# Rows spread over 64 partitions by way of DRAM: one copy read in one transfer, or eight copies read in one transfer for each head

## The chip, the cores and the metric

The kernel runs on one core of one Trainium2 chip. The metric is the device time of one execution in microseconds. Before the change three runs took 3809.49, 3809.7 and 3804.15 us; their median is 3809.49 us.

The engines go by short names here: PE is TensorE's matmul, PEld its weight load, DVE is VectorE, ACT is ScalarE, POOL is GpSimd, SP is SyncE. A `q` behind a name (`SPq`, `POOLq`) is the engine's sequencer, which issues DMA transfers.

## The reference

The input is an image batch of shape 4 x 32 x 32 x 768 in float32. Two residual layers follow each other. Each normalizes its input by groups of channels, computes q, k and v, and lets every position of an image attend to all 1024 positions in 12 heads of 64 channels. The scores get a bias that depends on the row and the column distance of the two positions. The core of both layers, cut to what matters:

```python
attn = einsum('bqc,bkc->bqk', q * scale, k)
attn = attn + rel_h[..., :, None] + rel_w[..., None, :]
attn = softmax(attn, axis=-1)
o = attn @ v
x = x + o @ w_proj + b_proj
```

Layer 0 takes q, k and v straight from a product with a weight matrix. Layer 1 sends them through a 3x3 convolution of each channel and a layer norm first, and adds q to `o` before the last product.

## The kernel before, in words

The work is cut into 48 items. An item is one image, one layer and one pair of heads, which fill the 128 partitions with 2 x 64 channels. The order is: layer 0 of images 0 and 1, layer 1 of images 0 and 1, then the same for images 2 and 3, with six pairs in each. `attend` (L720) handles an item in two halves of 512 queries. For each half it goes over the 1024 keys in two groups of four tiles of 128: PE makes the scores (L873) and adds the bias by a second product with `ones` (L875), ACT takes the exponential (L880), and PE sums the weighted values (L897). Nothing is divided at that point. The values leave as `weighed`, and the sum of the exponentials is divided out later.

The program's order on PE, DVE, ACT and POOL is written out by hand: `attend` yields after each stretch of work, and at each yield the pieces of the next item (its products, convolutions, norms, `positions`, `split`) are put into the instruction streams at the steps that `plan` (L643) names. `more` (L731) takes the next part of the division from the list `rest`. Most items of layer 0 compute the q, k and v of neighbours by seven products of half size in place of eight (`sevens`, L391); their PSUM tiles are `m4m`, `m3m`, `m1m` and `m` in the trace, and DVE adds their results (L412). `positions` (L598) makes the products `rel` (L613) that the bias is taken from. SP issues its DMA transfers in the program's order: weights (L250 to L263, L275 to L291, L928 to L929), inputs and outputs (L964, L974), and the transfers `z_inv` (L844) and `t` (L850) of the division. Two buffers hold the weights of the products, so a weight load is issued when PE has finished with the one before the last.

The division needs one number for each query and head, and needs it on the 64 partitions of the head. There are two ways:

- **Layer 0** (44 of 48 halves). DVE adds the exponentials of the key tiles (L889, L891), PE sums them over the partitions into four groups of 32 partitions with 256 queries each (L792), ACT and DVE make the inverse on 256 columns (L798 to L829), and every 32nd partition of it is written to the DRAM tile `z_inv` by SP (L844 in `spread`). One step later `call` reads it back into all 128 partitions of `t` (L850), each head's row 64 times. `spread_finish` (L853) multiplies on DVE (L856) and adds the bias of v on ACT (L864).
- **Layer 1** (47 of 48 halves, `by_ones`). The value matrix has a column of ones, so the sums come out of PE in row 63 of each head. `copy` (L744) writes the two rows to the DRAM tile `z` (L753) and reads them back into `t` (L754), both from POOL's queue. ACT then starts the inverse with `sums` (L806, L814, L815), and DVE refines and multiplies (L828, L829, L834, L837). `restore_last` (L763) sends the row that the ones had taken (L776).

The tile `t` has one buffer, and the two DRAM tiles have two each. The four remaining halves of layer 0 and the last half of layer 1 sum on the partitions directly (L811) and use no DRAM.

POOL's queue also carries the bias. `split` (L624) cuts it into a high part, `high` (L629), and what is left, `whole` (L630), and issues 16 transfers of 128 KB for each item (L640), 8 for each half of the queries, the high part first.

In `t<-z` and `t<-z_inv` the source is written as `z.unsqueeze(1).to_broadcast([2, D, QC])`: 2 rows outermost, each repeated 64 times, 512 elements long. In the bias transfers it is `some.unsqueeze(1).to_broadcast([D // 2, 2, QC])`: 32 rows outermost, each repeated twice.

## Time and profile before

| | before |
|---|---|
| runs, us | 3809.49, 3809.7, 3804.15 |
| profiled execution, us | 3810.16 |
| its span, first to last instruction, us | 3808.1 |
| mean granted TensorE clock | 0.998 |
| DVE, ACT, POOL busy | 64%, 46%, 14% |
| DMA, mean over the span | 90 GB/s |
| HBM read, written | 195.76 MB, 40.28 MB |
| `t<-z` (POOL) | 47 transfers of 256 KB, 7.9 us to landing |
| `t<-z_inv` (SP) | 44 transfers of 256 KB |
| `z<-weighed`, `z_inv<-z_inv` | 47 and 44 transfers of 4 KB |
| bias (POOL) | 768 transfers of 128 KB, 2.9 and 3.2 us to landing |

The profile comes from one execution on the chip. Its page gives each engine's busy time and share of the span, then the span in 40 slices with the granted TensorE clock in tenths, then groups of instructions by line. `t<-z` reads "written from `z` into `t`", and `xN` counts instructions. A list of waits names an engine and its line, then what ended the wait, then the total in us, the number of waits and the longest. A timeline row gives the start in us from the span's start, the length in us, the engine, the line and what it did; idle time ahead of it stands in brackets with what ended it. A row of a table of windows gives the stretch, its length, each engine's busy us (with the number of instructions), the granted clock, the mean busy share of the 16 DMA engines and GB/s. The trace also holds a record of every DMA packet with its queue, start, length and size; these are called packet records below.

The issue of a DMA on SP or POOL shows as an instruction of about 0.5 to 0.8 us on that engine's sequencer. A transfer's landing is counted from its issue.

### The profile page before, as it was taken

Reading aid. Unit: us, or ns where it says so; the run is one execution under the profiler, and the core shown is the slowest. Engines: PE = TensorE matmul, PEld = TensorE weight load, DVE = VectorE, ACT = ScalarE, POOL = GpSimd, SP = SyncE. Lnnn points to the kernel's source line nnn. Section 1 sums busy time; section 2 is a strip of 40 time slices with the busy share of each in tenths; the row PEclk is TensorE's granted clock in tenths of the full one; section 3 lists DMA queues with packets and bytes.
Section 4 is the critical chain, followed back from the end, with each engine's and each line's share of the span. In section 5 each row is a group of like instructions: output and inputs, shape, how many; then the busy total and the mean of one; then the engine's idle time right before and its main releaser. Section 6 shows DMA issues by size and latency. Waiting matters only on the chain.

```text
span 3808.1 us, 76869 instructions
## 1 busy us (share of the span) xinstructions
PE 3734.4 (98%) x33166; PEld 1655.9 (43%) x33166; DVE 2440.7 (64%) x3068; ACT 1750.4 (46%) x2573; POOL 526.2 (14%) x964
## 2 busy tenths in 40 slices
PE   8999999999999999999999999999999999999998
PEld 4635535534344444444535455355343444434442
DVE  2556554559678877688454554445586888867874
ACT  2455424545255553455534544254453555525562
POOL 0111100111111211111200010001111112111120
PEclk9999999999999999999999999999999999999999
DMA  4444543331431223311334232523214212142123
GB/s 149 113 131 117 145 136 105 112 92 45 121 100 48 58 59 95 123 48 49 83 115 127 61 87 68 176 68 83 58 50 131 85 50 66 46 122 66 48 58 100
DMA packets 220097, 342.17 MB, mean 90 GB/s; under 512 B 50654, under 2 KB 104138, under 8 KB 219752
## 3 DMA queue, kind: packets, MB, share of 16 engines
q1 hardware_dynamic: 128984, 223.58, 18.7%
q0 software_dynamic: 90768, 113.61, 12.5%
q8 instruction: 264, 4.33, 0.5%
q14 instruction: 81, 0.66, 0.1%
HBM read 195.76 MB, written 40.28 MB: 62 GB/s over the span
## 4 chain that ended last, share of the span: by engine, by line
PE 45%; DVE 5%; ACT 1%; DMA 1%; issue 1%; POOL 0%; DVEq 0%; SPq 0%; ACTq 0%; POOLq 0%
PE qkv L131 9%; PE s L873 8%; PE av L897 8%; PE m4m L131 3%; PE m1m L131 2%; PE m3m L131 2%; PE s L875 2%; PE p3p L131 2%; PE p4p L131 2%; PE p1p L131 2%; PE rel L613 1%; PE m L131 1%; DVE shared L544 1%; PE ln_c L556 1%; DVE acc L891 1%
## 5 line engine op out<-in xcount | busy, mean ns | idle before, releaser
L880 ACT ACTIVATE e<-s 128x1024 f32<-128x1024 f32 x768 | 775.0, 1024 | 426.2 <-PE s L875 396.2
L131 PE MATMUL qkv<-xn,wqkv_t 128*64 128x512 f32 x3648 | 814.3, 595 | 7.1 <-DVE gmean L334 2.6
L873 PE MATMUL s<-q,k 64*128 64x512 f32 x3072 | 811.4, 604 | 6.3 <-ACT e L880 3.9
L544 DVE SCALAR_TENSOR_TENSOR shared<-shared,sm 128x1056 f32<-128x1056 f32 x576 | 757.9, 1316 | 15.6
L875 PE MATMUL s<-bias,ones 64*128 64x512 f32 x1536 | 613.8, 791 | 7.0 <-DMA bias<-whole 7.0
L897 PE MATMUL av<-e,vt 128*64 128x512 f32 x2624 | 596.3, 596 | 0.0
L131 PEld LDWEIGHTS qkv<-xn,wqkv_t 128*64 128x64 f32 x3648 | 256.1, 137 | 482.6 <-issue 464.7
L640 POOL DMA_DIRECT2D bias<-high x384 | 202.7, 548 | 1798.7 <-ACT high L629 1561.1
L891 DVE TENSOR_TENSOR acc<-acc,e 128x1024 f32<-128x1024 f32 x294 | 360.1, 1225 | 114.3 <-ACT e L880 87.4
L873 PEld LDWEIGHTS s<-q,k 64*128 64x128 f32 x3072 | 281.5, 186 | 265.0 <-issue 214.3
L527 ACT ACTIVATE shared<-qkv,sm 128x512 f32<-128x512 f32 (+1 forms) x288 | 129.1, 501 | 467.9 <-PE qkv L131 467.9
L897 PEld LDWEIGHTS av<-e,vt 128*64 128x64 f32 x2624 | 185.6, 137 | 350.1 <-issue 317.5
L875 PEld LDWEIGHTS s<-bias,ones 64*128 64x128 f32 x1536 | 149.5, 187 | 191.3 <-issue 188.5
L640 POOL DMA_DIRECT2D bias<-whole x384 | 207.2, 571 | 48.2 <-DVE whole L630 31.1
L747 ACT COPY weighed<-av 128x512 f32<-128x512 f32 x96 | 56.3, 586 | 299.9 <-PE av L897 299.9
L559 DVE TENSOR_REDUCE mean<-ln_c 128x8 f32<-128x512 f32 x144 | 98.6, 685 | 107.5 <-PE ln_c L556 107.5
L889 DVE TENSOR_TENSOR acc<-e 128x1024 f32<-128x1024 f32 x49 | 60.0, 1224 | 167.6 <-PE z L792 128.0
L776 POOL DMA_DIRECT2D weighed<-last x94 | 50.6, 540 | 682.1 <-ACT last L773 679.1
L613 PEld LDWEIGHTS rel<-q,rel 64*32 64x32 f32 x6144 | 111.8, 105 | 58.8 <-issue 54.8
L613 PE MATMUL rel<-q_t,rel 64*32 64x32 f32 x6144 | 123.5, 195 | 2.5 <-issue 2.5
L613 PE MATMUL rel<-q,rel 64*32 64x32 f32 x6144 | 122.5, 195 | 0.8 <-issue 0.8
L131 PE MATMUL m3m<-xn,wqkv_t 128*64 128x512 f32 x528 | 120.9, 592 | 2.3 <-DVE shared L412 2.3
(172 smaller groups left out, 4289.3 us busy)
## 6 DMA issues: line engine op xcount, KB each, us to landing
bias<-high POOLq DMA_DIRECT2D x384, 128.0 KB, 2.9
bias<-whole POOLq DMA_DIRECT2D x384, 128.0 KB, 3.2
wqkv_t<-in_wqkv SPq DMA_DIRECT2D x78, 384.0 KB
wqkv_t<-mixed SPq DMA_DIRECT2D x66, 384.0 KB
wproj_t<-mixed SPq DMA_DIRECT2D x48, 384.0 KB
wqkv_t<-in_wqkv SPq DMA_DIRECT2D x66, 192.0 KB
xn<-in_x SPq DMA_DIRECT2D x24, 512.0 KB
x<-in_x SPq DMA_DIRECT2D x48, 256.0 KB
```

The lines of the kernel that those rows point to most:

```text
L131: nc.tensor.matmul(ps[lo : lo + D], a[:, lo : lo + D], b, start=start, stop=stop, **kw)
L527: nc.scalar.activation(self.pad[s][:, rows, there : there + src.shape[2]], src, AF.Identity, bias=col(self.column(s)))
L544: nc.vector.scalar_tensor_tensor(y, window, tap, y, ALU.mult, ALU.add)
L559: nc.vector.tensor_reduce(of, heads, AX.X, ALU.add)
L613: nc.tensor.matmul(ps[lo : lo + S, k * S : (k + 1) * S].rearrange("p (b c) -> p b c", b=2), rel[rows, 2 * self.layer + i, first : first + ...
L640: nc.gpsimd.dma_start(sets, some.unsqueeze(1).to_broadcast([D // 2, 2, QC]))
L873: nc.tensor.matmul(ps[:, j, :], k[rows, keys], q[rows, cols], start=True, stop=False)
L875: nc.tensor.matmul(ps[:, j, :], ones[rows, kt % 2 * P : (kt % 2 + 1) * P], bias[c][rows, kt // 2, :], start=False, stop=True,)
L880: nc.scalar.activation(e, ps, AF.Exp)
L889: nc.vector.tensor_tensor(acc, es[0], es[1], ALU.add)
L891: nc.vector.tensor_tensor(acc, acc, e, ALU.add)
L897: nc.tensor.matmul(av[j * D : (j + 1) * D, :], pair.vt[:, kt, j * D : (j + 1) * D], e[:, j, :], start=(kt == 0), stop=(kt == NKT - 1),)
```

## The change

Both DRAM tiles, `z` and `z_inv`, become eight times as large: `[2, 8, 512]` instead of `[2, 512]`. The writes fill all eight copies from the same rows. For `z` this stays one transfer; for `z_inv` it becomes one for each head, because the row of a head comes from two partitions with 256 columns each. The new helper `spread_rows` reads a head's eight copies into that head's 64 partitions, each copy eight times, and is called with POOL's queue in `copy` and with SP's in `call`. So `t` is filled by two transfers of 128 KB in place of one of 256 KB, and their source is 8 (repeated) x 8 copies x 512 elements. No arithmetic is changed, and nothing is moved to another step.

```diff
+COPIES = 8
...
+    def spread_rows(queue, t, z):
+
+        for j in range(2):
+            there = z[j].unsqueeze(0).to_broadcast([D // COPIES, COPIES, QC])
+            queue.dma_start(t[j * D : (j + 1) * D, :], there)
...
-                z = dram.tile([2, QC], F32, tag="z", name="z", bufs=2)
-                nc.gpsimd.dma_start(z, weighed[D - 1 :: D, :])
-                nc.gpsimd.dma_start(t, z.unsqueeze(1).to_broadcast([2, D, QC]))
+                z = dram.tile([2, COPIES, QC], F32, tag="z", name="z", bufs=2)
+                nc.gpsimd.dma_start(z, weighed[D - 1 :: D, :].unsqueeze(1).to_broadcast([2, COPIES, QC]))
+                spread_rows(nc.gpsimd, t, z)
...
-                z = dram.tile([2, QC], F32, tag="z_inv", name="z_inv", bufs=2)
-                nc.sync.dma_start(z.rearrange("j (h x) -> (j h) x", h=2), inv[S - 1 :: S, :])
+                z = dram.tile([2, COPIES, QC], F32, tag="z_inv", name="z_inv", bufs=2)
+                for j in range(2):
+                    rows = inv[(2 * j + 1) * S - 1 : (2 * j + 2) * S : S, :]
+                    there = z[j].rearrange("r (h x) -> h r x", h=2)
+                    nc.sync.dma_start(there, rows.unsqueeze(1).to_broadcast([2, COPIES, QC // 2]))
...
-                nc.sync.dma_start(t, z.unsqueeze(1).to_broadcast([2, D, QC]))
+                spread_rows(nc.sync, t, z)
```

## The prediction

> **What bounds the kernel now.** I read the page's busy shares first, then the PE waits, then who waits for the row transfers that the change touches, then the windows and the timeline around those waits.

> ```profile
> PE 3734.4 (98%) x33166; PEld 1655.9 (43%) x33166; DVE 2440.7 (64%) x3068; ACT 1750.4 (46%) x2573; POOL 526.2 (14%) x964
> ...
> PEclk9999999999999999999999999999999999999999
> ```

> TensorE is busy 98% of a span of 3808.1 us, so the change, which removes no matmul, can win only from the 74 us in which PE stands, and from its clock. The first 14 us of these are the first load. The PE waits (total us, times, longest) name most of the rest:

> ```profile
> PE warm L319 <- DMA xn<-in_x: 13.9, 1, 13.9
> ...
> PE s L875 <- DMA bias<-whole: 7.0, 4, 2.9
> ...
> PE rel L613 <- issue: 3.3, 3, 2.5
> ...
> PE m3m L131 <- DVE shared L412: 2.3, 1, 2.3
> ```

> No PE wait names the tile `t`. Its other waiters do, in DVE's and ACT's wait lists:

> ```profile
> DVE t L856 <- DMA t<-z_inv: 36.2, 6, 7.4
> ```

> ```profile
> ACT inv L806 <- DMA t<-z: 1.9, 1, 1.9
> ```

> How the transfer moves now stands in windows that hold little else (the last two columns are the mean busy share of the 16 DMA engines and GB/s). The first has `t<-z_inv` alone, the second only bias transfers:

> ```profile
> 276.00:279.80 3.80, 3.80 (x20) 1.29 (x18) 0.70 (x2) 0.00 (x0) 0.00 (x0) 1.00 0.13 51
> ...
> 3288.00:3290.50 2.50, 2.50 (x14) 0.86 (x12) 2.43 (x4) 0.00 (x0) 2.50 (x6) 1.00 0.92 250
> ```

> 0.13 of 16 is two engines: the 256 KB, whose source has 2 rows outermost, crawl on two engines at 25 GB/s each. The bias transfers, 32 rows outermost, use all 16. The issue table says the same: `t<-z` 256 KB lands in 7.9 us, bias 128 KB in 2.9 to 3.2. The packet records of `t<-z_inv` show 128 packets of 2 KB, 0.085 us each, 64 in a row on each of two engines: 5.4 us.

> **Where this reaches PE.** Six times `t<-z_inv` is issued just as the 16 bias transfers go out, and shares its two engines with them. It then lands 10.0 to 11.0 us after its issue (packet records) instead of 6.5 to 7.8, DVE stands for it, and the bias transfers, which use the same two engines among their 16, land in 6 to 8 us. One of the six in the timeline, PE's row and DVE's (start, length, and in brackets the idle time before and what ended it):

> ```profile
> 254.71 0.50 PE L875 MATMUL s<-bias,ones 64*128 64x512 f32 x2 [2.35 <-DMA bias<-whole]
> ```

> ```profile
> 259.14 0.69 DVE L856 TENSOR_TENSOR t<-weighed,t 128x512 f32<-128x512 f32 x1 [4.08 <-DMA t<-z_inv]
> ```

> The four bias waits of PE are 0.74 (385.05), 2.35 (254.71), 2.92 (2142.10) and 0.98 (2581.88). The last three lie behind such a collision; at 385 the transfer, issued at 382.93, was not yet moving. After the two long ones the clock falls:

> ```profile
> 255.00:260.00 5.00, 5.00 (x20) 2.65 (x17) 0.75 (x2) 3.07 (x3) 0.90 (x2) 0.66 0.65 196
> ...
> 1818.00:1823.00 5.00, 3.82 (x14) 2.24 (x16) 4.76 (x10) 1.30 (x4) 5.00 (x11) 0.66 0.97 242
> 2143.00:2148.00 5.00, 5.00 (x25) 2.48 (x22) 0.69 (x1) 3.13 (x4) 0.52 (x1) 0.66 0.33 78
> ```

> 5 us at 0.66 is 1.7 us lost. Waits of 0.98 and 2.34 us left it at 1.00 in their windows.

> **The change, part by part.** *The read of `t`.* Two transfers of 128 KB, each with 8 rows outermost, repeated, in place of one of 256 KB. No row has 8. From the side of speed the bias row bounds a half at 2.9 us; from the other, 7.9 us as now. I take about 3.4 for both halves, 2.9 and one further issue of 0.5: if the engines used follow the outermost rows, as with 2 and 32, 8 engines at 25 GB/s carry 128 KB in 0.64 us. [...]

> *The write of `z` and `z_inv`.* 16 packets of 2 KB, or two transfers of 16 of 1 KB, for 2 or 4 packets. If one row stays on one engine, 8 packets of 0.085 us: +0.6 us; between 0 and +1.5, what the bias row of 3.2 lies above the 1.7 of `z`. Taken: 0.6 on POOL, 0.4 on SP.

> *Issues.* SP has two more per use (0.52 each), 44 times, and waits for the second write: `t` is issued some 1.0 us later on SP and 0.6 on POOL, its second half 0.5 later still. Behind the waiting SP stand the halves of `t`, then weight loads. In the common pattern (274.42) SP's next issue follows 5.4 us later and itself waits for PE, which covers it. At six places (447.67, 527.65, 892.88, 1970.06, 2412.02, 2777.89) it follows after 0.6 to 2.4 us; were the weights there just in time, that is 6 x 1.5 = 9 us, but PE's only wait for weights in the whole run is 0.9 us. POOL has 47 issues of 0.84 turned into two of about 0.55, and a `z` write of 0.58 or a little more: 0.3 to 0.6 us, ahead of issues that come 5 us later (idle 4.95 before `weighed<-last` at 1806.26). Both at nothing.

> *The gains, in terms.*
> 1. Bias waits. PE needed the bias at 252.36, 2139.18 and 2580.90; the last transfer of that half was issued at 248.7, 2135.5 and 2577.2. With the undisturbed 3.2 us it is there at 251.9, 2138.7 and 2580.4, ahead each time; with 16 packets of `t` on an engine in front (16 x 0.085 = 1.4) up to 0.9 late. So 6.25 us are won at best, 3.55 at worst; I take the middle, 4.9.
> 2. The clock behind the two long ones: 2 x 1.7 = 3.4.
> 3. At 394 DVE stood 5.79 us for `t`, and PE's m3m then 2.34 for DVE. `z_inv` left at 379.87; 3.1 us to the first read today, 1.0 for the longer front, then 1.75 to the first packet and twice 1.4 us of packets shared with bias give 388.5 to 389 against DVE's readiness at 388.68: 2.3 won.
> 4. At 1807.81 ACT waited 1.85 us for `t<-z`. Its twin at the end of the other half of the batch did not wait:

> ```profile
> 1807.81 0.63 ACT L806 ACTIVATE inv<-t 128x512 f32<-128x512 f32 x1 [1.85 <-DMA t<-z]
> ...
> 3683.92 0.63 ACT L806 ACTIVATE inv<-t 128x512 f32<-128x512 f32 x1
> ```

> PE then stood 2.47 us ahead of `rel` (1810.18), in the twin 0.53, and the clock fell in the first place only: 1.94 + 1.7 = 3.6. With the change `t` lands by 1804.6 (issue 1801.1, then 3.4), before ACT is free at 1805.96. What is late next there is ACT's own chain, as in the twin.

> Sum 4.9 + 3.4 + 2.3 + 3.6 = 14.2 us. The profiled execution took 3810.16, so 3796.0; the median of the runs, 3809.49, lies 0.7 lower: **3795.3**.

> **The rivals.**
> *Bias is its own bound.* The 16 bias transfers hold 0.92 of the engines by themselves; terms 1 and 2 might stay, only 3 and 4 come: 3809.5 - 5.9 = 3803.6. For it: the 0.92. Against it: undisturbed bias lands in 2.9 to 3.2.
> *The halves aren't spread* (copies folded into one source, or placed on the same two engines). If the longer front is hidden too, the time stays 3809.5. If it isn't, *slower*: `t` lands 1.5 us later at five places where it already binds (the three bias waits, m3m, 1808), so 7.5 us, and the waits of 0.98 and 2.34 us grow into clock falls, 3.4 more: 3820. This decides as soon as the landing of `t` passes today's. For it: no row shows 8. [...]

> **How the numbers follow.** 0.2%, 7.6 us, is about what a measurement of this kernel can tell from no change. Forecast 0.64, bias its own bound 0.16, not spread and hidden 0.10, not spread and slower 0.10. The forecast's own range is 3790 to 3802: all of term 1 and 2 us of other waits more, or half of the terms. The range reaches to the bias rival and stops short of the slow one: 3789 to 3807. Faster 0.64, same 0.26, slower 0.10.

> **What would show it.** In windows with `t` alone a DMA share of about 0.5 instead of 0.13; `t<-z` landing in about 3.4 us; DVE's wait for `t<-z_inv` down from 36.2 us to under 4; PE's for bias under 3.5; no 0.66 at these three places; ACT at 1808 not waiting. It is wrong if `t` lands as late as today, or if PE waits for weights.

## The result and the profile after

| | before | after |
|---|---|---|
| median of 8 runs each, us | 3808.89 | 3793.51 |
| lowest to highest, us | 3804.15 to 3811.64 | 3790.87 to 3797.78 |
| profiled execution and its span, us | 3810.16, 3808.1 | 3790.87, 3788.9 |
| PE standing still, gaps over 0.15 us, us | 65.8 | 55.7 |

The ratio is 0.9964, with a 95% interval of 0.9955 to 0.9973: faster by 0.36%, or 15.4 us between the medians where 14.2 were forecast. Line numbers are 3 to 12 higher in the changed kernel (L613 is now L616, L856 is L868, L875 is L887, L806 is L815); its reads of `t` are L725.

The page of the kernel after, the lines that answer to those shown of before:

```profile
PE 3725.5 (98%) x33166; PEld 1651.2 (44%) x33166; DVE 2442.2 (64%) x3068; ACT 1750.2 (46%) x2573; POOL 545.0 (14%) x1011
...
PEclk9999999999999999999999999999999999999999
```

Its list of waits (engine, line, what ended the wait, then total us, times, longest):

```profile
PE warm L322 <- DMA xn<-in_x: 12.4, 1, 12.4
...
DVE t L868 <- DMA t<-z_inv: 9.1, 5, 2.7
...
PE rel L616 <- issue: 2.2, 1, 2.2
...
PE s L887 <- DMA bias<-whole: 1.6, 1, 1.6
```

DVE's wait for `t` fell from 36.2 to 9.1 us and PE's for bias from 7.0 to 1.6; m3m and ACT's `inv` no longer wait. The `rel` wait is still there, and it says "issue", not the name of an engine: this matters below. PE is busy 8.9 us less with the same 33166 matmuls, of which the clock explains most.

The read of `t` by itself, on POOL's queue, in the windows table (busy us of PE, PEld, DVE, ACT, POOL, then granted clock, DMA share, GB/s). First before, in a window in which almost every packet belongs to one `t`:

```profile
1301.00:1305.00 4.00, 3.76 (x24) 2.01 (x24) 3.90 (x6) 3.57 (x5) 0.00 (x0) 1.00 0.14 56
```

then after, in a window that holds nothing but the 64 packets of two halves:

```profile
1184.60:1186.20 1.60, 1.60 (x10) 0.31 (x6) 0.67 (x2) 0.00 (x0) 0.00 (x0) 1.00 0.51 146
```

0.14 of 16 engines is two. The 0.51 is an average, and the eight has to be read from the packet records of this window: eight packets of 4 KB are under way while one half moves, and 16 to 18 for the 0.3 us in which both do. So each half moves on eight engines, and on POOL's queue the second half uses eight others than the first. The issue tables, before and then after (size, median us from issue to landing), show what that does to one transfer:

```profile
t<-z POOLq DMA_DIRECT2D x47, 256.0 KB, 7.9
...
z<-weighed POOLq DMA_DIRECT2D x47, 4.0 KB, 1.7
```

```profile
t<-z POOLq DMA_DIRECT2D x94, 128.0 KB, 3.2
...
z<-weighed POOLq DMA_DIRECT2D x47, 32.0 KB, 2.3
```

The packet records agree: after an issue before, there are 64 packets of 4 KB and 448 of 8 bytes, which fits 32 for each of 14 engines that carry nothing; after, the two halves leave 64 of 8 bytes, which fits 4 for each of 8 idle engines, twice. On SP, 2 packets of 2 KB were under way at once (3 at most), now 8 (10 at most). It stays at 8 where both halves are issued together (at 849.3), so there they share the same eight. The prediction's estimate, worked out from the 2 and the 32 rows of before, held: here 8 rows outermost gave 8 engines.

The stall shown at 254.71 has shrunk to nothing for PE. DVE's timeline of after (start, length, idle time before in brackets) at the same multiply:

```profile
253.88 0.69 DVE L868 TENSOR_TENSOR t<-weighed,t 128x512 f32<-128x512 f32 x1 [0.59 <-DMA t<-z_inv]
```

and the windows of after near the three places where the clock had been at 0.66 (the whole trace of after has no fall of the clock but the one at the program's end):

```profile
254.00:259.00 5.00, 5.00 (x32) 1.73 (x32) 4.25 (x4) 3.03 (x8) 0.00 (x0) 1.00 0.75 231
...
1818.00:1823.00 5.00, 3.58 (x20) 1.33 (x19) 4.24 (x9) 3.64 (x6) 1.14 (x2) 1.00 0.18 33
2141.00:2146.00 5.00, 5.00 (x26) 1.72 (x24) 1.59 (x4) 2.89 (x4) 0.00 (x0) 1.00 0.16 44
```

**Where 19.2 us of span went.** PE's gaps are 10.1 us shorter and its busy time 8.9. Of the gaps, 5.4 are bias waits (three gone, 6.25; that at 385 grew by 0.85), 2.3 m3m, 0.7 net the two ends of layer 1, 1.5 the first load. Of the busy time, 6.8 are four falls of the clock that are gone (at 256, 1819, 2143 and 3754), each recorded as 3.413 us at half speed, so 1.7 lost. This execution is the fastest of the eight after, and the medians differ by 15.4 only: the first load and two of the four falls come and go, as the experiments show.

### The profile page after: what moved, and what is told of

Its sections match the earlier page's. It is cut to its first block, busy times and chain, and to the rows that moved or that the text cites. A ratio compares the mean times of both kernels' runs of the same rounds, so it can differ in the third digit from the quotient of the medians.

```text
span 3788.9 us, 77201 instructions
## 1 busy us (share of the span) xinstructions
PE 3725.5 (98%) x33166; PEld 1651.2 (44%) x33166; DVE 2442.2 (64%) x3068; ACT 1750.2 (46%) x2573; POOL 545.0 (14%) x1011
## 3 DMA queue, kind: packets, MB, share of 16 engines
q1 hardware_dynamic: 130832, 224.84, 19.2%
## 4 chain that ended last, share of the span: by engine, by line
PE 88%; DVE 8%; ACT 2%; issue 1%; DMA 1%; SPq 0%; POOL 0%; DVEq 0%; ACTq 0%
PE qkv L134 19%; PE s L885 16%; PE av L909 16%; PE m4m L134 5%; PE m1m L134 5%; PE m3m L134 5%; PE s L887 4%; PE p3p L134 3%; PE p4p L134 3%; PE rel L616 3%; PE p1p L134 2%; PE m L134 2%; DVE shared L547 2%; PE ln_c L559 1%; DVE acc L903 1%
## 5 line engine op out<-in xcount | busy, mean ns | idle before, releaser
L887 PE MATMUL s<-bias,ones 64*128 64x512 f32 x1536 | 611.3, 789 | 1.6 <-DMA bias<-whole 1.6
L887 PEld LDWEIGHTS s<-bias,ones 64*128 64x128 f32 x1536 | 148.6, 187 | 184.1 <-issue 176.3
L616 PEld LDWEIGHTS rel<-q,rel 64*32 64x32 f32 x6144 | 111.7, 105 | 60.6 <-issue 56.5
L616 PE MATMUL rel<-q,rel 64*32 64x32 f32 x6144 | 122.4, 195 | 2.4 <-issue 2.2
L616 PE MATMUL rel<-q_t,rel 64*32 64x32 f32 x6144 | 123.4, 195 | 0.0
L134 PE MATMUL m4m<-xn,wqkv_t 128*64 128x512 f32 x528 | 121.7, 596 | 1.5 <-ACT z_inv L808 1.4
```

The lines of the kernel that those rows point to most:

```text
L134: nc.tensor.matmul(ps[lo : lo + D], a[:, lo : lo + D], b, start=start, stop=stop, **kw)
L616: nc.tensor.matmul(ps[lo : lo + S, k * S : (k + 1) * S].rearrange("p (b c) -> p b c", b=2), rel[rows, 2 * self.layer + i, first : first + ...
L887: nc.tensor.matmul(ps[:, j, :], ones[rows, kt % 2 * P : (kt % 2 + 1) * P], bias[c][rows, kt // 2, :], start=False, stop=True,)
```

## The experiments

**Theory:** `t` is slow because 2 rows outermost hold it at two engines, and these two also delay the bias transfers; the rows outermost are what counts, and the gain comes at the SP reads of layer 0 (terms 1 to 3) and the POOL reads of layer 1 (term 4). **Rivals:** the copies help, because 64 partitions no longer read one address; two transfers in flight help; or one half of the change does everything. All ratios are to the kernel before on the same chip, whose median was 3805.98, 3807.95 and 3806.23 us on the three chips used (E1 to E4, E5 to E8, E9 to E11).

**E1 and E2, each half alone.** E1 leaves POOL's `z` and `t` as they were, E2 SP's.

```diff
 E1
-                z = dram.tile([2, COPIES, QC], F32, tag="z", name="z", bufs=2)
-                nc.gpsimd.dma_start(z, weighed[D - 1 :: D, :].unsqueeze(1).to_broadcast([2, COPIES, QC]))
-                spread_rows(nc.gpsimd, t, z)
+                z = dram.tile([2, QC], F32, tag="z", name="z", bufs=2)
+                nc.gpsimd.dma_start(z, weighed[D - 1 :: D, :])
+                nc.gpsimd.dma_start(t, z.unsqueeze(1).to_broadcast([2, D, QC]))
```

> Only layer 0's transfers are changed (z_inv in eight copies, t<-z_inv as two transfers); layer 1's z and t are as before. Theory (t leaves its two engines, so bias and DVE no longer wait): the bias waits of PE stay near 1.6 us, DVE's wait for t<-z_inv near 9 us, the wait of 2.34 us at m3m is gone, so 7.7 us of stalls plus clock falls: about 3798 us, 11 us under before, and ACT's 1.85 us wait at the end of layer 1 is back. Rival (layer 1's half is what counts, by the end of each half of the batch): 3804 or above.

> Only layer 1's transfers are changed (z in eight copies, t<-z as two transfers); layer 0's are as before. Theory: ACT's wait of 1.85 us goes, PE wins 1 to 2 us there and perhaps one clock fall of 1.7 us: 3805 to 3808 us; the bias waits of 7.0 us, DVE's 36 us and m3m's 2.34 us stay. Rival: most of the gain is here, 3798 us.

E1 took 3795.97 us, ratio 0.9977 (0.9968 to 0.9986), 10.0 us won. E2 took 3803.97, ratio 0.9991 (0.9982 to 1.0), 2.0 us won, which is at the edge of what can be told from nothing. The waits of E1:

```profile
DVE t L868 <- DMA t<-z_inv: 8.6, 5, 2.4
ACT inv L815 <- DMA t<-z: 2.3, 1, 2.3
PE rel L616 <- issue: 2.3, 2, 2.0
...
PE s L887 <- DMA bias<-whole: 0.7, 1, 0.7
```

and of E2:

```profile
DVE t L865 <- DMA t<-z_inv: 35.8, 6, 7.6
...
PE s L884 <- DMA bias<-whole: 5.2, 3, 2.4
PE rel L616 <- issue: 3.0, 2, 2.5
PE m3m L134 <- DVE shared L415: 2.6, 1, 2.6
```

Each half removes its own waits and leaves the other's. The `rel` line is new knowledge: in E1 ACT waits 2.3 us for `t<-z` and PE stands 2.0 there, in E2 ACT does not wait and PE stands 2.5. PE's `rel` wait does not come from ACT's.

**E3, one copy, 64 rows outermost.** The writes are those of before; each head's single row is read 64 times with the repetition outermost.

```diff
-            there = z[j].unsqueeze(0).to_broadcast([D // COPIES, COPIES, QC])
+            there = z[j : j + 1, :].to_broadcast([D, QC])
```

> z and z_inv stay single copies written as before; only the read is cut into two transfers, one for each head, each with 64 repeated rows outermost, so that all rows of a transfer read the same 2 KB. Theory (the outermost dimension sets the engines, not the addresses): 64 on both sides gives 16 engines, t lands about as early as with eight copies or earlier, and one write of 4 KB is shorter than what eight copies need: 3790 to 3794 us. Rival A (the copies matter, reads of one address queue up): t lands in 6 us or more and the time goes back towards 3805 or above. Rival B (splitting by head alone is what helps): the same time as with eight copies, but a DMA share that stays at two engines.

3793.82 us, ratio 0.9973 (0.9963 to 0.9982), 12.2 us won: the whole gain of E1 and E2 together, without any copy. Its issue table and waits:

```profile
t<-z POOLq DMA_DIRECT2D x94, 128.0 KB, 2.8
...
z<-weighed POOLq DMA_DIRECT2D x47, 4.0 KB, 1.7
```

```profile
DVE t L865 <- DMA t<-z_inv: 1.1, 1, 1.1
PE s L884 <- DMA bias<-whole: 0.8, 1, 0.8
```

A half lands 0.4 us earlier than with eight copies, the front is shorter, and DVE's wait falls to 1.1 us. No packet of 8 bytes is recorded, which fits 16 engines that all carry. So reading one row 64 times does not undo the gain, and the rival of the addresses falls as the cause. It is not free: with four copies, 16 rows outermost (E8), a half lands in 2.5 us, 0.3 earlier, and most often 16 of its packets are under way at once, where with one copy it is mostly 6 to 13. In the kernel's time this can't be seen.

**E4, 32 copies.** Only `COPIES = 32`, which makes 2 rows outermost again.

> The changed kernel with 32 copies in place of eight: two transfers again, but the source is 2 (repeated) x 32 copies x 512. Theory: back to two engines, each transfer of 128 KB at 51 GB/s, and a longer write: t lands as late as before or later, DVE's wait for t<-z_inv is 36 us or more, PE's bias waits 6 us or more: 3808 to 3822 us. Rival A (different addresses are what helps): as fast as with eight copies, 3794 us. Rival B (the split by head helps): also near 3794 us.

3886.87 us, ratio 1.0217 (1.0203 to 1.0231): 81 us slower, far beyond what was expected, 3822 at most. Two engines came back as expected (448 packets of 8 bytes, 5.9 us for each half), but the write of `z` grew as well (128 KB, 4.4 us), and then SP's order did damage that the prediction had put at nothing. SP's timeline of E4:

```profile
706.44 1.08 SPq L856 DMA_DIRECT2D z_inv<-z_inv  x2
711.68 0.50 SPq L725 DMA_DIRECT2D t<-z_inv  x1
726.79 0.34 SPq L266 DMA_DIRECT2D wqkv_t<-mixed  x1
727.18 0.52 SPq L725 DMA_DIRECT2D t<-z_inv  x1
```

DVE and PE in the same stretch:

```profile
733.08 0.69 DVE L868 TENSOR_TENSOR t<-weighed,t 128x512 f32<-128x512 f32 x1 [19.73 <-DMA t<-z_inv]
```

```profile
738.22 4.53 PE L134 MATMUL m3m<-xn,wqkv_t 128*64 128x512 f32 x10 [8.90 <-DVE shared L415]
```

The second half of `t` stands behind a weight load (L266) that SP could not issue for 14.6 us; SP's waits name PE's m3m matmuls as what usually holds L266. DVE waits 19.7 us for that half, and PE in turn 8.9 for DVE. The span is 75.0 us longer than before's: PE's gaps make 52.5 of it (three such circles of 8.7 to 8.9 us, and bias waits of 22.9 in all), and its busy time 22.5, with 13 falls of the clock against 4. E4 changes engines, write and order at once, so it doesn't price the two engines alone; E7 and E9 do.

**E5 and E11, the changed kernel again**, on two other chips:

> The changed kernel unchanged, on the same chip as its neighbours here. Theory: 12 to 16 us under before on this chip, ratio 0.996 to 0.997. A ratio beside that of the single-copy kernel (0.9973) within the intervals would say that the copies themselves bring nothing.

> The changed kernel, unchanged, beside the one with a single copy on one chip: ratio 0.995 to 0.9975. The clock falls near 1803 and near 3680 to 3755 come and go between executions if they are not tied to t; if they are tied to it, none is seen there.

3792.54 us, ratio 0.9954 (0.994 to 0.9968), and 3792.41, ratio 0.996 (0.9946 to 0.9974). The bias wait at 380 is 0.7 us in both, as before the change, so the 1.6 of the first execution is no effect of it. The clock near 1801 and 3680, in the windows of E5 and then of E11:

```profile
1801.00:1806.00 5.00, 3.86 (x41) 1.94 (x41) 4.76 (x5) 4.91 (x7) 0.69 (x2) 1.00 0.02 3
3676.00:3682.00 6.00, 4.48 (x18) 2.33 (x18) 5.76 (x10) 2.75 (x5) 6.00 (x13) 0.72 0.97 227
```

```profile
1799.00:1806.00 7.00, 4.72 (x54) 2.40 (x42) 6.53 (x8) 6.50 (x9) 0.98 (x2) 0.64 0.02 5
3676.00:3682.00 6.00, 4.47 (x18) 2.15 (x16) 5.72 (x11) 2.27 (x5) 6.00 (x13) 0.72 0.94 223
```

One kernel, three executions: at 1801 no fall, no fall, a fall of 6.8 us; at 3678 none, one, one. PE stood the same 2.2 to 2.3 us at `rel` each time. The falls at the ends of layer 1 are therefore not tied to `t`. The two behind the bias waits (256 and 2143) are: none of the eight executions with SP's reads on 8 or 16 engines has one there. With the slow read such falls stay, but they change places: at 254, 400 and 701 in E2, at 2269 in E7, at 2266 in E9, each time at a bias or m3m wait.

**E6, eight copies in one transfer.**

```diff
-                spread_rows(nc.sync, t, z)
+                nc.sync.dma_start(t, z.unsqueeze(2).to_broadcast([2, COPIES, D // COPIES, QC]))
```

(and the same on POOL's queue)

> z and z_inv in eight copies as in the change, but t is read in one transfer of 256 KB with 2 rows outermost, each of the eight copies eight times: other addresses, same outermost dimension as before. Theory (engines): t stays on two engines at 51 GB/s, its front is longer by 0.5 to 1 us, DVE's wait for t<-z_inv stays at 36 us or grows to 45, the bias waits stay: 3806 to 3818 us. Rival A (reading eight addresses is what helps): as fast as the change, about 3793 us.

3793.03 us, ratio 0.9957 (0.9943 to 0.9971). The premise of the expectation failed: this does not hold the read at two engines. The issue table and a window that holds only one such transfer:

```profile
t<-z POOLq DMA_DIRECT2D x47, 256.0 KB, 3.2
```

```profile
1292.70:1293.70 1.00, 1.00 (x12) 1.00 (x10) 0.80 (x2) 0.60 (x1) 0.00 (x0) 1.00 0.62 225
```

0.62 on average is more than 8 of 16, up to 18 packets are under way at once, and the read leaves no 8-byte packet (the 56 of each use belong to the write of `z`): [2 heads][8 copies] lie one behind the other in DRAM and act as 16 rows. So E6 is no test of the addresses (E3 is). It shows that the split into two transfers isn't needed: DVE's wait is 4.9 us, against 9.4 for the changed kernel on this chip, and the times agree within their intervals. On 16 engines each, the kernel took 3793.03 us with one transfer and 3792.51 with two (E8). The split gains nothing here; what the copies bring is more engines, as the 7.7 us of the same write read from copy 0 alone (E9) beside the 3.2 here show.

**E7, the split alone.** Two copies, outermost, each repeated 32 times, in one transfer for each head.

```diff
-COPIES = 8
+COPIES = 2
...
-            there = z[j].unsqueeze(0).to_broadcast([D // COPIES, COPIES, QC])
+            there = z[j].unsqueeze(1).to_broadcast([COPIES, D // COPIES, QC])
```

> Two copies, and two transfers of 128 KB, one for each head, with the 2 copies outermost, each repeated 32 times: the change's split, but with 2 outermost. Theory (engines): each half runs on two engines, 51 GB/s, on SP both on the same two, and where weight loads slip in between the halves the second half is later still: t as late as before or later, 3806 to 3840 us. Rival B (the split by head is what helps): as fast as the change, about 3793 us.

3813.19 us, ratio 1.001 (1.0001 to 1.0019). DVE's wait is 38.4 us, PE's for bias 8.8 and for m3m 4.8, and 448 packets of 8 bytes are back:

```profile
t<-z POOLq DMA_DIRECT2D x94, 128.0 KB, 5.2
```

```profile
DVE t L868 <- DMA t<-z_inv: 38.4, 6, 7.1
```

Two transfers on two engines each were no better here than one.

**E8, four copies**, so 16 rows outermost (`COPIES = 4`):

> The changed kernel with four copies: 16 (repeated) x 4 copies x 512, so 16 outermost and a shorter write. Theory: 16 engines, t<-z lands in 2.8 to 3.2 us, DVE's wait for t<-z_inv falls from 9 us to 1 to 5 us, the time is that of eight copies or up to 3 us less. Rival (a larger number of copies is what helps): slower than with eight copies, by a part of the gain, 3797 to 3802 us.

3792.51 us, ratio 0.9957 (0.9943 to 0.9971); a half lands in 2.5 us, `z` in 2.0, DVE waits 2.0 us. 16 engines were worth no more than 8 for the time (3792.54 in E5, on the same chip): what PE still waits for isn't `t`.

**E9, the new write with the old read**, from copy 0:

```diff
-                spread_rows(nc.sync, t, z)
+                nc.sync.dma_start(t, z[:, 0, :].unsqueeze(1).to_broadcast([2, D, QC]))
```

(and the same on POOL's queue)

> The new write (eight copies, and its second issue on SP) with the old read of 256 KB in one transfer from copy 0, 2 rows outermost. Theory (the 2 rows outermost hold the read at two engines, whatever the copies): t<-z lands in 7.9 us as before, DVE's wait for t<-z_inv is 36 us or up to 6 us more for the later issue, PE's bias waits 7 to 9 us, m3m 2.3 to 4, ratio 1.000 to 1.003. Rival (the longer front costs at five places 1.5 us each and two clock falls): ratio 1.003 or more. Rival (the copies themselves help): bias waits under 4 us and ratio 0.998 or less.

3808.54 us, ratio 1.0007 (0.9998 to 1.0016). `t<-z` lands in 7.7 us, DVE waits 42.6 us, and the waits of PE only move (7 to 9 us were expected for bias, 2.3 to 4 for m3m):

```profile
PE s L887 <- DMA bias<-whole: 5.2, 2, 4.4
PE m3m L134 <- DVE shared L415: 4.6, 3, 2.2
```

The copies and their second write on SP cost between nothing and 0.16% by themselves; the rival's 0.3% or more is excluded.

**E10, one copy beside the changed kernel on one chip:**

> The kernel with one copy and 64 repeated rows outermost once more, now on one chip with the changed kernel. Theory (the copies bring nothing, the rows outermost do): within 0.1% of the changed kernel's ratio, DVE's wait for t<-z_inv at 0 to 3 us against its 9. Rival (the copies are worth something beyond the engines): slower than the changed kernel by more than 0.1%.

3792.72 us, ratio 0.9961 (0.9948 to 0.9975), against E11's 0.996. The two can't be told apart, though DVE waits 1.5 us for `t` in one and 8.7 in the other. No version beat the changed kernel measurably; the one with a single copy is the smaller, with 4 KB written where the changed kernel writes 32.

## Why the prediction was right, point by point

- **Which uses bind.** The prediction read that `t<-z_inv` meets the bias transfers six times. The packet records of before show at least 16 uses that do, each landing 8.8 to 11.0 us after its issue. What sets the six apart is DVE: its multiply comes 10.5 to 11.5 us after the issue there, and 14.9 us or more in the other ten.
- **The read of `t`.** 8 engines for each half and a share near 0.5 were forecast; 0.51 was measured, as an average of 8 and 16. 3.4 us for both halves was a little short: a half lands in 3.2, and the second is issued 0.58 later, so 3.8.
- **The longer front** (what comes between the numbers leaving and the read of `t`). +0.6 on POOL was measured as 1.7 to 2.3 us; on SP the first half of `t` follows `z_inv` by 2.23 us in the pattern below, where it was 1.69, so 0.5 in place of 1.0. The issues cost PE nothing here, as forecast, but the reason given was incomplete. SP did not keep to the program's order, as was assumed ahead of the prediction: `spread_rows` issues the two halves one behind the other, but in the changed kernel weight loads came between them in 28 of 44 uses. SP's timeline of after shows one:

```profile
266.64 1.10 SPq L856 DMA_DIRECT2D z_inv<-z_inv  x2
268.86 0.61 SPq L725 DMA_DIRECT2D t<-z_inv  x1
273.71 0.33 SPq L256 DMA_DIRECT2D wqkv_t<-in_wqkv  x1
274.09 0.42 SPq L257 DMA_DIRECT2D wqkv_t<-in_wqkv  x1
274.61 0.62 SPq L725 DMA_DIRECT2D t<-z_inv  x1
```

  The second half starts 5.75 us behind the first. It is harmless there because in those uses the multiplies come 14.6 us or more after `z_inv` is issued; in the six uses where DVE needs `t` early (8.5 to 9.9 us behind `z_inv`) the halves go together. E4 shows the bill where they don't. The prediction asked what waits behind `t`, and not what may slip in front of its second half.
- **Term 1, bias waits, 4.9 of 3.55 to 6.25.** The three waits are gone completely: 6.25, the upper end. The halves are not out of the way by then: they still meet the bias transfers, but more briefly. The last transfer of the half that PE needed landed 6.2 to 7.3 us after its issue before, and 3.8 to 5.1 after. That is later than the undisturbed 3.2, and still early enough. The rival that bias is its own bound is excluded by the 0.7 us left in E1, E5 and E11.
- **Term 2, the clock behind them, 3.4.** Both falls are gone in every variant with SP's reads on 8 or 16 engines.
- **Term 3, m3m, 2.3.** It is gone. Terms 1 to 3 were 10.6 together; E1, which holds just these, won 10.0.
- **Term 4, the end of layer 1, 3.6.** This failed in part. ACT's wait of 1.85 is gone, as forecast, but not PE's stall ahead of `rel`. The PE rows with idle time there, before:

```profile
1810.18 0.19 PE L613 MATMUL rel<-q_t,rel 64*32 64x32 f32 x1 [2.47 <-issue]
...
1814.17 1.13 PE L873 MATMUL s<-q,k 64*128 64x512 f32 x4 [1.22 <-ACT whole L619]
1816.29 1.13 PE L873 MATMUL s<-q,k 64*128 64x512 f32 x4 [0.76 <-ACT e L880]
1819.18 1.94 PE L556 MATMUL ln_c<-cst,shared 128*128 128x128 f32 x8 [1.52 <-ACT ln_ln L153]
```

  and after:

```profile
1802.08 0.21 PE L616 MATMUL rel<-q,rel 64*32 64x32 f32 x1 [2.23 <-issue]
...
1806.54 1.13 PE L885 MATMUL s<-q,k 64*128 64x512 f32 x4 [0.61 <-ACT e L892]
...
1809.43 1.06 PE L559 MATMUL ln_c<-cst,shared 128*128 128x128 f32 x8 [1.53 <-ACT ln_ln L156]
```

  The stall ahead of `rel` falls inside a run of 256 recorded `rel` matmuls, after the 234th before and the 233rd after, and stays at 2.0 to 2.8 us in all of E1 to E11 but E7 (1.7), whether ACT waits or not. "issue" meant what it says: no other engine released it. What did is in the packet records of one more DMA queue, here as the page of before lists it (packets, MB, share of the 16 engines' span):

```profile
q8 instruction: 264, 4.33, 0.5%
```

  These are packets of 16 KB, one for every 255 instructions that PE and PEld start (67227 in all), so they appear to bring PE's program. In before one runs from 1807.53 to 1808.87 and PE's stall ends at 1810.18, 1.3 us later; in after one ends at 1800.75 and the stall at 1802.08. All 85 stalls of PE over 0.15 us that are named "issue", in all 13 executions, end 1.2 to 1.6 us behind the end of such a packet; of the 766 other stalls 9 do. In before PE and PEld had started 513 instructions in the 6.5 us since the packet ahead of it, two packets' worth. The reading that fits is that PE waits there for its own instructions, and that `t` has no part in it. No run changed how instructions are brought, so this rests on that agreement in time.

  What goes with ACT's wait are the stalls behind it, 1.22 and 0.76, of which 0.61 is left; that ACT's wait caused them is likely but not shown (E4, with a wait of 1.6, has 0.39 there). The four sum to 5.97 before and 4.37 after: 1.6 us won where 1.94 were forecast, from other rows than those named; and in this execution the other end of layer 1 grew by 0.9 (gaps over 0.15 us up to `ln_c`: 3.05 to 3.98). The fault was to take the twin, whose `rel` stall is 0.53, as proof that ACT made the difference. The 1.7 us of clock counted here are chance. E2, which holds just this term, won 2.0 in place of 3.6.
- **The sum.** By halves 10.0 + 2.0 = 12.0 us on one chip, where E3 won 12.2; the changed kernel won 13.8 and 15.4 on two chips more and 15.4 in the first comparison. 14.2 lies among them, with term 1 sized too small and term 4 too large. That these two errors nearly cancel, 1.35 against 1.6 to 2.0, is luck. The forecast's lower end of 3790 does not follow from its terms either: all of term 1 and 2 us more give 3792.
- **The rivals.** "The halves aren't spread" would have been cheaper than its 10.5 us: E9, the longer front with one read on two engines, costs 2.3 (at most 6.1), and E7, two halves on two engines each, 5.2 between the medians (at most 7.2). The five places were not each delayed by 1.5: with `t` issued later in E9 the collisions fell elsewhere (a bias wait of 4.4 at 2267, none at 254 or 2142).

## What to carry to other kernels

The broadcast read was here as fast as its outermost rows let it be spread: 256 KB landed in 7.9 us with 2 rows, and each half of 128 KB in 3.2 with 8, 2.5 with 16 and 2.8 with 64. Look for a low DMA share in a window of its own (0.13 and 0.14 here, two engines of 16), and try the loop order before copies, since 64 repeats of one row outermost (E3) did as well as eight copies. The slow transfer on two engines cost most through what it delayed on them: 36 us of DVE waits were worth little by themselves, and the bias, m3m and clock terms were worth 10. PE's stall ahead of `rel`, named "issue", was not explained by its neighbour's wait, however near in time (2.0 us with ACT's wait in E1, 2.5 without it in E2), and the twin with 0.53 proved nothing: for such a stall, look in the packet records of the queue that the page calls instruction.
